# A floor under the issue time of token loads and packed-weight loads, and unpacking two places later, in a one-core attention and FFN layer

## The chip, the cores and the metric

The kernel runs on one core of a Trainium2 chip. The metric is the device time of one execution in microseconds (us). Three runs of the kernel before gave 826.74 us in the median (825.87 to 827.88). PE is the matrix engine (PEld its weight loads), DVE the vector engine, ACT the scalar engine, POOL the general-purpose engine, and SP the queue from which nearly all DMAs of this kernel are issued, in order.

## The reference

The layer takes tokens `x` of 4 batches x 512 positions x 1024 channels and computes, in fp32:

```
x = x + attention(layernorm(x))          # 32 query heads of 32 channels, one shared key/value head
x = x + layernorm(x) @ W.T + bias        # W is 1024 x 1024, stored packed

attention: q = n @ Wq ; k, v = split(n @ Wkv)
           p = softmax(q k^T / sqrt(32) + slope_h * (pos_k - pos_q), causal)
           out = (p v) @ Wo
W:         qweight is int32 [1024, 768]; each group of 3 words gives 4 codes of 6 bits:
           v0 = w0 & 63, v1 = (w0 >> 6) & 63, v2 = w1 & 63, v3 = w2 & 63
           W = (code - zero_point[row]) * scale[row]
```

The packed weights do not depend on the tokens. They are unpacked, turned and written back to device memory (`wf_d`) at any time before the FFN reads them.

## The kernel before

**Stages.** The attention is cut into 32 steps: 4 batches x 8 groups of 4 heads. A step `i` is `queries(at, i)` (24 products `pq`, L682, which use the two-part split of weights and tokens for accuracy), a round trip of the queries through device memory (`q_d`) into a tile `qs` (L697 to L714, all recorded at the helper line L420), `maxima(at, i)` (products `s`, L738, whose row maxima DVE takes at L751 into `mx`), a transpose of the maxima `trm` (L767), two small DMAs of them into `qs` (`qs<-mt`), and `attention(at, i)` (products `st` L819, exponentials on ACT L829, causal masking L838 and sums L860 on POOL, products `pav` L848 and `den` L877). After the steps come 16 token tiles with the output projection (`po` L1047) and the FFN (`pf` L1167).

**Tokens of a batch.** `load_x` brings four tiles of 128 tokens (512 KB each, L554) into the pool `x`, which has 4 buffers. `layernorm` takes their statistics on DVE (L527), the reciprocal root on POOL, and normalizes on ACT (L585, later batches). `chunk` transposes them on PE (L598) and splits them into eight tiles `xc_b_c`, which `keys_values` and all eight `queries` of the batch read. `load_x` of batches 1 to 3 has a nominal place of `T - 45 + 3 t` us, where `T = 16 + 120 b` is that of the batch's first step.

**Unpacking.** `unpack(at, c)` handles 128 rows of the packed weights: a load `qw` (384 KB, L908), three shift/mask operations on DVE (`v`, L912, L919, L926), a conversion on ACT (`code`, L934), a transposing DMA (`across`, L942), another conversion on ACT (`codes`, L945), and a write to `wf_d` (512 KB, L948, recorded at L420). `qw`, `v` and `codes` take buffers of the pool `xc`. That pool has 10 buffers, 8 of which hold the tokens of the current batch, so two are to spare.

**What sets the order.** No order is written out by hand. Every operation is entered with an engine, a modelled cost and a nominal place `at`; `Work.order` then runs a list scheduler over it. A forward pass puts on each engine the ready operation that is wanted first; a DMA is held back until `o.hold`, and from the second pass on also until 12 us (`EARLY`) before the latest time that a backward pass gave it. The backward pass knows nothing of holds, and both passes charge DMAs to a modelled rate. Of 4 rounds of up to 7 forward passes the one with the earliest modelled end wins, and that order is issued on every engine. `o.hold` is 0 except for DMAs issued from POOL, which are held to their `at`. Nominal places, holds and the planned start times are on the planner's clock, which is near the trace's but not the same: the keys and values of batch 1 have the nominal place 135 us and run at 145 us in the trace.

Which buffer a tile takes is decided by `slots`, from the nominal places in the first round and from the planned starts in later rounds. Each engine executes its own list strictly in the planned order, so one late operation holds back all behind it on its engine, SP's DMA issues included.

Of the kernel before, what the change touches and what calls it, by code (L numbers as in the profile page):

```python
# [336 lines left out]
STEP = 15.0  # L337
# [4 lines left out]
def layer_kernel(  # L342
# [14 lines left out]
    nc = tc.nc  # L357
# [3 lines left out]
    NG = NH // GH  # L361
# [4 lines left out]
    work = Work()  # L366
# [14 lines left out]
    def new(pool_name, tag, shape, dt, name):  # L381

        p, bufs = pools[pool_name]
        return work.item(lambda: p.tile(shape, dt, tag=tag, name=name), (pool_name + tag, bufs))
# [13 lines left out]
    def act(at, n, fn, out, ins, sbuf=False):  # L398
        work.op("ACT", at, n / 1.2 + (90.0 if sbuf else 70.0), fn, out, ins)

    def dve(at, n, fn, out, ins, port=False, more=0.0):
        work.op("DVE", at, n / 0.96 + 75.0 + more, fn, out, ins, port=port)
# [1 line left out]
    def pool_op(at, cost, fn, out, ins):  # L404
        work.op("POOL", at, cost, fn, out, ins, port=True)

    def dma(at, size, fn, out, ins, eng="SP"):
        work.op(eng, at, 0.0, fn, out, ins, size=size)

    def split(at, n, hi, lo, src, hi_it, lo_it, src_it, port=False):  # L410

# [7 lines left out]
    def move(dst, src):  # L419
        return nc.sync.dma_start(out=dst.bitcast(F32), in_=src.bitcast(F32))  # L420
# [22 lines left out]
        out=mask(),  # L443
        in_=mask(),
# [14 lines left out]
    def prep_keys(at, i):  # L459
        dma(  # L460
            at, 61e3, lambda: nc.gpsimd.dma_start(out=kst[i]()[R_BIAS:R_ALL, :], in_=k_rows),
            [(kst[i], "b")], [], eng="POOL",
        )

    def prep_rows(at, g):
        dma(
            at, 229e3, lambda: nc.gpsimd.dma_start(out=qr_d[g], in_=q_rows[g]), [qr_i[g]], [],
            eng="POOL",
        )
# [4 lines left out]
    def prep_wkv(at):  # L474
        st = new("stg", "stg", [P, KC, 2 * HD], F32, "wkv_st")
        src = w_kv.rearrange("(c p) d -> p c d", p=P)
        dma(at, 262e3, lambda: nc.sync.dma_start(out=st(), in_=src), [st], [])
        split(
            at + 18.0, HALF, lambda: wkv()[:, :, 0 : 2 * HD], lambda: wkv()[:, :, 2 * HD :], st,
            (wkv, 0), (wkv, 1), st, port=True,  # L480
        )
# [68 lines left out]
    def load_x(at, b, t):  # L550
        xt = xh[b, t] = new("x", "x", [P, H], F32, f"x_{b}_{t}")
        src = x[b, ts(t, P), :]
        if b or t < NT - 1:
            dma(at, 524e3, lambda: nc.sync.dma_start(out=xt(), in_=src), [xt], [])  # L554
            return
        for i in range(2):
            dma(
                at + 0.001 * i, 262e3,
                lambda i=i: nc.sync.dma_start(out=xt()[:, ts(i, HALF)], in_=src[:, ts(i, HALF)]),
                [(xt, i)], [],  # L560
            )
# [342 lines left out]
    def unpack(at, c):  # L904

        qw = new("xc", "xc", [P, H // 4, 3], I32, f"qw_{c}")
        src = qweight[ts(c, P), :].rearrange("p (g w) -> p g w", w=3)
        dma(at, 393e3, lambda: nc.sync.dma_start(out=qw(), in_=src), [qw], [])  # L908
        v = new("xc", "xc", [P, H // 4, 4], I32, f"v_{c}")
        dve(  # L910
            at + 4.0, 256,
            lambda: nc.vector.tensor_scalar(  # L912
                v()[:, :, 0:1], qw()[:, :, 0:1], 63, None, ALU.bitwise_and
            ),
            [(v, 0)], [qw], port=True,
        )
        dve(
            at + 4.0, 256,
            lambda: nc.vector.tensor_scalar(  # L919
                v()[:, :, 1:2], qw()[:, :, 0:1], 6, 63, ALU.logical_shift_right, ALU.bitwise_and  # L920
            ),
            [(v, 1)], [qw], port=True,
        )
        dve(
            at + 4.0, 256,
            lambda: nc.vector.tensor_scalar(  # L926
                v()[:, :, 2:4], qw()[:, :, 1:3], 63, None, ALU.bitwise_and
            ),
            [(v, 2)], [qw], port=True,
        )  # L930
        code = new("stg", "stg", [P, H], BF16, f"code_{c}")
        act(
            at + 5.0, H,
            lambda: nc.scalar.activation(  # L934
                code(), v().rearrange("p g j -> p (g j)"), AF.Copy, bias=-CODE_MID
            ),
            [code], [v], sbuf=True,
        )
        across = new("stg", "stg", [P, KC, P], BF16, f"across_{c}")
        dma(  # L940
            at + 6.0, 700e3,
            lambda: nc.sync.dma_start_transpose(out=across(), in_=code()), [across], [code],  # L942
        )
        turned = new("xc", "xc", [P, KC, P], F32R, f"codes_{c}")
        act(at + 12.0, H, lambda: nc.scalar.copy(turned(), across()), [turned], [across], sbuf=True)  # L945
        dma(
            at + 14.0, 600e3,
            lambda: move(wf_d.rearrange("k p n -> p k n")[:, :, ts(c, P)], turned()),  # L948
            [(wf_i, c)], [turned],
        )  # L950
# [266 lines left out]
    T0 = 16.0  # L1217
    for t in range(NT):
        load_x(0.01 * t, 0, t)
        layernorm(1.0 + t, 0, t)  # L1220
# [4 lines left out]
        prep_wq(2.0 if g == 0 else T0 + (g - 0.9) * STEP, g)  # L1225
        prep_rows(T0 + g * STEP + (2.0 if g == 0 else -6.0), g)
    for c in range(KC):
        unpack(T0 + (1.6 + 2.0 * (c % 3) + NG * (c // 3)) * STEP, c)
    for b in range(B):
        T = T0 + b * NG * STEP  # L1230
        if b:
            for t in range(NT):
                load_x(T - 3.0 * STEP + 3.0 * t, b, t)
            for t in range(NT):
                layernorm(T - 2.0 * STEP + 3.0 * t, b, t)
        for c in range(KC):
            chunk(
                T - 4.0 + 0.5 * c if b == 0 else T - 0.9 * STEP + 1.3 * c - 2.6, b, c
            )
        keys_values(T + 6.0 if b == 0 else T - 1.0, b)  # L1240
        for g in range(NG):
            i = b * NG + g
            at = T0 + i * STEP
            queries(at, i)
            maxima(at + 17.0, i)
            attention(at + 34.0, i)
        invert(T + NG * STEP + 48.0, b)
# [52 lines left out]
```

## Time and profile before

| | |
|---|---|
| median of 3 runs | 826.74 us |
| the profiled execution | 825.42 us |
| its span, first to last instruction | 823.5 us |
| PE busy | 795.9 us (97%) |
| DVE, ACT, POOL busy | 565.5, 372.3, 514.1 us |
| moved by DMA | 133.39 MB, 162 GB/s over the span |
| granted TensorE clock, mean | 0.994 |

The span is the profiled execution from its first to its last instruction; its own time is 1.92 us longer. The chain of waits that ended last goes through PE for 89% of the span. Idle time of PE is therefore what there is to read: 27.6 us in all, and its place in the span tells what would have to arrive earlier. Where two engines, or an engine and the DMAs, run side by side, only the one that PE waits for counts. A granted clock below 1.00 makes PE's products longer without any idle time.

### The profile page before, as it was taken

What the parts mean: (1) busy time and instruction counts of PE and PEld (TensorE: products, weight loads), DVE (VectorE), ACT (ScalarE), POOL (GpSimd) and SP (SyncE); (2) the same over time, 40 slices, a digit from 0 to 9 for tenths busy, and PEclk for the clock granted to TensorE, in tenths of its full rate; (3) what the DMA queues carried; (4) which work ended last, traced back from release to release, by engine and by line L of the source; (5) the groups of instructions that cost most, each with busy time, mean ns of one, the idle gap of its engine ahead of it and who ended that gap; (6) DMA issues with size and microseconds to landing.
All of it is one profiled execution on the core that took longest, in us unless ns stands there. A gap on an engine that the chain in (4) does not pass through costs nothing.

```text
span 823.5 us, 13425 instructions
## 1 busy us (share of the span) xinstructions
PE 795.9 (97%) x4480; PEld 594.7 (72%) x4480; DVE 565.5 (69%) x1491; ACT 372.3 (45%) x659; POOL 514.1 (62%) x442
## 2 busy tenths in 40 slices
PE   5979999999999999999999999999999999999997
PEld 4756676777676767676775767667888888888885
DVE  7476777388786388777367675644998666666865
ACT  4336575464775445675556564330233323332320
POOL 4337977276787375877489896879465445554333
PEclk9989999999999999999999999999999999999999
DMA  7885853395553387543567966526875755665321
GB/s 223 245 252 154 232 164 91 111 266 188 155 145 100 106 262 211 148 120 111 174 174 194 235 189 208 170 58 171 214 178 158 173 131 129 152 151 137 97 52 51
DMA packets 131796, 133.39 MB, mean 162 GB/s; under 512 B 42964, under 2 KB 93140, under 8 KB 130704
## 3 DMA queue, kind: packets, MB, share of 16 engines
q1 hardware_dynamic: 130912, 129.01, 57.0%
q0 software_dynamic: 816, 3.53, 1.7%
q8 instruction: 35, 0.57, 0.3%
q14 instruction: 33, 0.27, 0.1%
HBM read 85.58 MB, written 39.85 MB: 152 GB/s over the span
## 4 chain that ended last, share of the span: by engine, by line
PE 89%; DVE 4%; DMA 2%; ACT 2%; issue 1%; POOL 1%; SPq 1%; DVEq 0%; ACTq 0%; POOLq 0%
PE po L1047 21%; PE pq L682 21%; PE pf L1167 13%; PE st L819 9%; PE s L738 9%; PE pav L848 8%; PE den L877 4%; PE pkv L616 2%; PE tr L598 2%; DVE junk L751 2%; ACT p L829 1%; POOL p L860 1%; DMA wo_st<-in_L_attn_Wo_dram 1%; DMA qs<-mt 1%; SPq L420 1%
## 5 line engine op out<-in xcount | busy, mean ns | idle before, releaser
L751 DVE CUSTOM_DVE_ANT_0 junk<-s,mask 128x384 f32<-128x384 f32 (+3 forms) x512 | 250.6, 490 | 119.6 <-PE s L738 88.8
L860 POOL TENSOR_TENSOR p<-p,p 128x1536 f32<-128x1536 f32 (+2 forms) x96 | 232.4, 2421 | 16.7 <-PE pav L848 15.0
L829 ACT ACTIVATE p<-st 128x512 f32<-128x512 f32 (+1 forms) x352 | 183.9, 559 | 115.8 <-PE st L819 110.7
L682 PE MATMUL pq<-xc,wqh 128*128 128x512 f32 x512 | 198.5, 405 | 2.3 <-DVE ql L415 1.4
L1047 PE MATMUL po<-woh,aT 128*128 128x512 f32 x512 | 164.8, 391 | 0.0
L838 POOL TENSOR_SCALAR_AFFINE_SELECT p<-p 128x512 f32<-128x512 f32 x128 | 82.2, 647 | 105.1 <-ACT p L829 104.3
L738 PE MATMUL s<-kst,qs 124*128 124x384 f32 (+3 forms) x512 | 127.5, 324 | 3.9 <-DVE mx L751 3.6
L819 PE MATMUL st<-qs,kst 126*128 126x512 f32 (+1 forms) x352 | 127.1, 399 | 3.9 <-ACT p L829 2.9
L1167 PE MATMUL pf<-wf,xT 128*128 128x512 f32 x512 | 121.1, 390 | 0.7 <-DVE xT L415 0.7
L738 PEld LDWEIGHTS s<-kst,qs 124*128 124x128 f32 x512 | 91.5, 189 | 34.2 <-DVE mx L751 8.9
L682 PEld LDWEIGHTS pq<-xc,wqh 128*128 128x128 f32 x512 | 97.7, 191 | 23.8 <-issue 2.7
L1047 PEld LDWEIGHTS po<-woh,aT 128*128 128x128 f32 x512 | 96.1, 188 | 21.7 <-DVE mx L751 0.8
L1167 PEld LDWEIGHTS pf<-wf,xT 128*128 128x128 f32 x512 | 95.8, 188 | 20.9 <-DVE xT L415 1.1
L682 PE MATMUL pq<-xc,wql 128*128 128x512 f32 x256 | 101.8, 398 | 0.1
L1047 PE MATMUL po<-wol,aT 128*128 128x512 f32 x256 | 99.7, 389 | 0.0
L819 PEld LDWEIGHTS st<-qs,kst 126*128 126x128 f32 x352 | 63.5, 190 | 25.7 <-ACT p L829 10.8
L848 PE MATMUL pav<-p,kv 128*32 128x512 f32 (+3 forms) x1024 | 79.9, 436 | 0.0
L848 PEld LDWEIGHTS pav<-p,kv 128*32 128x32 f32 x1024 | 29.6, 109 | 48.8 <-issue 37.6
L1187 POOL TENSOR_TENSOR x<-x,y 128x512 f32<-128x512 f32 x30 | 42.7, 1425 | 27.4 <-DVE y L1178 27.4
L1047 PEld LDWEIGHTS po<-wol,aT 128*128 128x128 f32 x256 | 48.1, 188 | 9.6
L538 POOL TENSOR_SCALAR rstd_f<-mv_f 128x1 f32<-128x1 f32 x16 | 3.9, 244 | 81.7 <-DVE mv_f L533 72.7
L682 PEld LDWEIGHTS pq<-xc,wql 128*128 128x128 f32 x256 | 49.2, 192 | 7.2 <-POOL wql L489 0.6
(92 smaller groups left out, 878.6 us busy)
## 6 DMA issues: line engine op xcount, KB each, us to landing
qs<-q_d SPq DMA_DIRECT2D x96, 256.0 KB
x<-_attn_hidden_states_dram SPq DMA_DIRECT2D x31, 512.0 KB
q_d<-qh SPq DMA_DIRECT2D x32, 256.0 KB
q_d<-ql SPq DMA_DIRECT2D x32, 256.0 KB
at_d<-a SPq DMA_DIRECT2D x32, 256.0 KB
raw<-at_d SPq DMA_DIRECT2D x16, 512.0 KB
raw<-rden_d SPq DMA_DIRECT2D x64, 128.0 KB
out_dram<-x SPq DMA_DIRECT2D x32, 256.0 KB
```

Of the source, the lines that this page charges most:

```text
L682: nc.tensor.matmul(pq(), w()[:, c, :], xc[b, c]()[:, s, :], start=(c == 0 and n == 0), stop=(c == KC - 1 and n == 2),)
L738: nc.tensor.matmul(ps()[:, o : o + W], q()[0:R_MAX, at, ts(t, P)], k()[0:R_MAX, :W], start=True, stop=True,)
L751: lambda ps=ps, junk=junk, t=t, h=h, W=W, o=o: nc.vector.tensor_tensor_reduce(out=junk()[:, :W], in0=ps()[:, o : o + W], in1=mask()[:, S - ...
L819: nc.tensor.matmul(ps()[:, place, :], k()[0:R_ALL, ts(j, P)], q()[0:R_ALL, mine, j * P :], start=True, stop=True,)
L829: lambda ps=ps, own=own, j=j: nc.scalar.activation(pr[j]()[:, own, :], ps(), AF.Exp),
L838: nc.gpsimd.affine_select(out=d, in_=d, pattern=[[0, GH], [1, P]], compare_op=ALU.is_ge, fill=0.0, base=0, channel_multiplier=-1,)
L848: nc.tensor.matmul(pav()[ts(h, HD), j * P :], kv[b]()[:, j, HD:], pr[j]()[:, h, :], start=(j == 0), stop=(j == NT - 1), tile_position=(0, ...
L860: nc.gpsimd.tensor_tensor(d, d, pr[j](), ALU.add)
L877: nc.tensor.matmul(d()[ts(h, HD), :], onesel()[:, g, :], pr[0]()[:, h, :], start=(g == 0), stop=(g == NG - 1), tile_position=(0, h * HD),)
L1047: nc.tensor.matmul(po(), aT[s][1]()[:, c, :], w()[:, ts(n, HALF)], start=(c == 0 and m == 0), stop=(c == KC - 1 and m == 2),)
L1167: nc.tensor.matmul(pf(), xT()[:, s, c, :], wf[c]()[:, ts(n, HALF)], start=(c == 0 and s == 0), stop=(c == KC - 1 and s == 1),)
L1187: (nc.vector if last else nc.gpsimd).tensor_tensor(d, d, y(), ALU.add)
```

## The change

`dma` takes an optional `hold`, in us on the planner's clock, before which the planner may not issue it. Two kinds of DMA get one:

- the token tiles of batches 1 to 3: `at - 37.5` us, which is 53.5, 56.5, 59.5 and 62.5 us for batch 1, 173.5 to 182.5 for batch 2, 293.5 to 302.5 for batch 3;
- the packed weights `qw`: `at - 3.0` us.

The nominal places of the eight unpackings are counted from `c + 1` instead of `c`. In steps of 15 us after `T0 = 16` they were 1.6, 3.6, 5.6, 9.6, 11.6, 13.6, 17.6 and 19.6; they become 3.6, 5.6, 9.6, 11.6, 13.6, 17.6, 19.6 and 21.6. The floors of the eight `qw` loads are thus 67, 97, 157, 187, 217, 277, 307 and 337 us. Nothing is added to or taken from the work itself: the same instructions and DMAs are issued. The order in which the planner puts them can change anywhere.

```diff
-    def dma(at, size, fn, out, ins, eng="SP"):
-        work.op(eng, at, 0.0, fn, out, ins, size=size)
+    def dma(at, size, fn, out, ins, eng="SP", hold=None):
+
+        o = work.op(eng, at, 0.0, fn, out, ins, size=size)
+        if hold is not None:
+            o.hold = hold * 1e3
...
         if b or t < NT - 1:
-            dma(at, 524e3, lambda: nc.sync.dma_start(out=xt(), in_=src), [xt], [])
+            dma(
+                at, 524e3, lambda: nc.sync.dma_start(out=xt(), in_=src), [xt], [],
+                hold=at - 2.5 * STEP if b else None,
+            )
             return
...
-        dma(at, 393e3, lambda: nc.sync.dma_start(out=qw(), in_=src), [qw], [])
+        dma(at, 393e3, lambda: nc.sync.dma_start(out=qw(), in_=src), [qw], [], hold=at - 3.0)
...
     for c in range(KC):
-        unpack(T0 + (1.6 + 2.0 * (c % 3) + NG * (c // 3)) * STEP, c)
+        unpack(T0 + (1.6 + 2.0 * ((c + 1) % 3) + NG * ((c + 1) // 3)) * STEP, c)
```

## The prediction

> **What bounds the kernel now.** I read the engine shares first, then the busy time by stretches to find where PE is idle or slow, then who PE waited for, and last the SP queue and the DVE in the stretch that stood out.
>
> ```profile
> PE 795.9 (97%) x4480; PEld 594.7 (72%) x4480; DVE 565.5 (69%) x1491; ACT 372.3 (45%) x659; POOL 514.1 (62%) x442
> ```
>
> PE has 823.5 - 795.9 = 27.6 us without work. In stretches of 6 us the start of the kernel looks like this (each engine's busy time, then the granted PE clock, the DMA share, GB/s):
>
> ```profile
> 28.00:34.00 6.00, 4.55 (x23) 3.43 (x22) 1.07 (x3) 3.24 (x6) 0.48 (x1) 1.00 0.98 237
> 34.00:40.00 6.00, 5.86 (x27) 4.47 (x26) 4.01 (x13) 1.24 (x2) 3.83 (x4) 1.00 1.04 350
> 40.00:46.00 6.00, 2.88 (x14) 1.94 (x14) 5.40 (x23) 1.36 (x3) 1.27 (x1) 0.99 1.08 294
> 46.00:52.00 6.00, 6.00 (x20) 4.87 (x21) 3.16 (x9) 1.77 (x2) 3.80 (x8) 0.73 1.04 332
> 52.00:58.00 6.00, 4.04 (x18) 2.64 (x18) 4.85 (x17) 3.36 (x4) 2.35 (x4) 1.00 0.58 148
> 58.00:64.00 6.00, 5.43 (x20) 4.09 (x19) 4.49 (x20) 2.66 (x5) 0.64 (x1) 0.72 0.58 169
> ```
>
> PE is idle for 1.45 + 0.14 + 3.12 + 1.96 + 0.57 = 7.24 us between 28 and 64 us, and two stretches run at a clock of 0.73 and 0.72, which lengthens their products by (0.27 + 0.28) x 6 = 3.30 us. Together 10.54 us. From 28 to 52 us the DMA engines are full. Of the rest of the idle time some 8 us lie before the first product, 5.5 us after 800 us (neither is touched), and about 5 us are spread over 64 to 580 us in waits of at most 0.8 us.
>
> ```profile
> PE st L819 <- ACT p L829: 2.6, 7, 0.5
> PE trm L767 <- DVE xc L415: 0.8, 2, 0.5
> PE st L819 <- DMA qs<-mt: 0.8, 1, 0.8
> ```
>
> So a moved DMA can win only in the first 64 us, and can lose anywhere later. This is SP's list in the full stretch (start, duration of the issue):
>
> ```profile
> 33.86 0.43 SPq L554 DMA_DIRECT2D x<-_attn_hidden_states_dram  x1
> ...
> 35.25 0.98 SPq L554 DMA_DIRECT2D x<-_attn_hidden_states_dram  x2
> ...
> 40.50 0.38 SPq L420 DMA_DIRECT2D wf_d<-codes  x1
> 41.36 4.31 SPq L908 DMA_DIRECT2D qw<-in_L_ffn_qweight_dram  x1
> 45.76 0.54 SPq L507 DMA_DIRECT2D wq_st<-in_L_attn_Wq_dram  x1
> 46.40 1.70 SPq L420 DMA_DIRECT2D q_d<-qh  x1
> 48.19 0.42 SPq L420 DMA_DIRECT2D q_d<-ql  x1
> 48.70 1.25 SPq L420 DMA_DIRECT2D qs<-mt  x2
> ```
>
> The reader should see three token tiles of batch 1 (1.5 MB, not normalized by ACT before 49 us, not transposed before some 110 us), a write of unpacked codes (0.5 MB), and a packed load whose issue blocks SP for 4.31 us. Behind them stand the queries and maxima that PE needs: the maxima were ready on DVE at 46.5 us, were issued at 48.70, and the first `st` product ran at 57.93.
>
> **The change, part by part.** *Which floors bind.* The packed loads are issued at 5.3, 41.4, 83.7, 160.3, 193.9, 216.7, 290.0 and 322.1 us; the floors are 67, 97, 157, 187, 217, 277, 307 and 337. The first two move by 62 and 56 us, the third by 73, the rest by 15 to 60. Token tiles of batch 1 are issued at 33.9, 35.3, 35.7 and 71.2 against floors of 53.5 to 62.5, so three move by 20 to 24 us. Batches 2 and 3 (issued 167 to 197 and 291 to 310) have floors at most 7 us later than that: no effect worth a number.
>
> *What leaves the first 64 us.* Unpacking 0 takes with it the SP issues of 3.29, 1.73 (transposing DMA at 24.79) and 0.38 us, three DVE operations (20.11 to 23.58), and 2.1 us of ACT; unpacking 1 its issue of 4.31 us and 1.2 us of DVE at 62; the three token tiles 1.4 us of SP issue, about 4 us of statistics on DVE between 41.5 and 49, 3 us on POOL, and 3.6 us of ACT. In bytes: 0.77 MB packed, 0.25 MB transposed, 0.5 MB of codes, 1.5 MB of tokens, some 3 of the 14.4 MB that move before 60 us.
>
> *What then comes sooner.* The low part of the first queries (`ql`) waits behind the DVE unpacking: its ACT half is done at 22.42, it starts at 23.50. That is 1.1 us. Its path to `qs` is behind the 1.73 us transposing issue and in a stretch with a DMA share of 0.98. The first `s` product ran at 34.62. It cannot run before the keys are copied, at 30.17 (ACT, 29.58 + 0.58), so the gain there is at most 34.62 - 30.2 = 4.4 us; I take most of it. The PE wait at 31.7 (1.45 us) then has `s` products to fill it. DVE needs 9.9 us for sixteen maxima (35.06 to 45.0), so these end near 41 instead of 45. The small DMAs of the maxima took 4.8 us on the chain of waits in a later stretch (318.44, 4.82); from an issue at 42 that makes the first `st` at about 47, not 57.9. Until then PE has the products of queries 2 and 3 (5.5 us each) and of two sets of maxima.
>
> *What stays.* While no `st` is there, PE runs at DVE's pace: five waits on the maxima between 53 and 60 us (0.53, 0.34, 0.55, 0.54, 0.54) sum to 2.50 us. I keep 2.50 as idle, and one of the two slow-clock stretches (1.65). Gain at the start: 10.54 - 2.50 - 1.65 = 6.4 us; its ends are 0 (DVE bounds the fill as now, below) and 10.54.
>
> *What it costs later.* The same work now lies beside full PE work. One unpacking is 2.3 us of SP issue (0.64 + 1.28 + 0.40), 2.2 us of DVE in the median (single operations up to 3.70 us at 165 us, beside POOL), and 2.1 us of ACT; DVE is 69% and ACT 45% busy, so this is hidden as long as no maxima or queries queue right behind it. Rows for it exist: 300 to 340 us holds a packed load, three token tiles and a transposing DMA, and PE loses 1.46 us there, against 0.0 to 0.5 in its neighbours. Bounds: nothing, or less than nothing since three unpackings leave places where a `st` waits now, to eight times the 0.81 us wait for the maxima's DMA at 323 = 6.5 us. I take 1.0, since the stretches from 140 to 260 us, which hold three unpackings, lose 0.48 + 0.04 + 0.41 = 0.93 in all. If the cover goes (a maxima operation behind a 3.7 us DVE operation), one such event costs up to 3 us.
>
> *Sum.* 6.4 - 1.0 = 5.4 us. The profiled execution of 825.42 us (span 823.5 + 1.92) would become 820.0; it stands 1.32 below the median of the runs, so the forecast is 826.74 - 5.4 = **821.3 us**.
>
> *Two rules against the rows.* The Trainium skill, "DMA: Bandwidth & Descriptors", section "Rules for kernel authors", advises to issue a DMA early and wait late so that its cost overlaps; by it the early loads are free, the gain is nothing, and only the cost of 1.0 us is left: 827.7. The 4.31 us issue and the share of 1.04 to 1.08 speak against it here. "TensorE: Matmul & The Clock Gate", Part 1, has the clock halve after an idle window of about 3.4 us; the waits of 40 to 46 us are 1.68 us at the longest, and the clock still fell to 0.73. By the rule no clock loss could be won back and the forecast would be 1.65 us higher, 823.0.
>
> **The rivals.** *DVE bounds the fill.* For: in the 40 to 46 stretch DVE is 5.40 of 6 us busy and every PE wait there names the maxima. Against: DVE is idle for 5 of 6 us from 28 to 34, so a start 4 us sooner costs it nothing. Then only the 1.45 us wait goes, 1.0 is paid later: 826.3.
>
> *The last unpacking meets the batch switch (slower).* Unpacking 7 takes 35.7 us from load to write now (322.05 to 357.78). From its floor of 337 it ends at 373 or later, holding one or two of the ten `xc` buffers, while the tokens of batch 3 are turned into theirs from 356 and 369.6 to 389. If a `chunk` copy waits for that write, the queries of step 24 wait behind it on PE, which has at most a step's rest to do. The same can befall unpacking 4 at the switch near 255. Price: 8 us (8 of the 16 us of overlap); 826.74 - 5.4 + 8 = 829.3. It decides for slower from a wait of 7.1 us on. Against: the places of 5.6 and 13.6 steps already hold unpackings before two switches, with no wait on PE above 0.4 us at either.
>
> *The floors do nothing.* Excluded: eleven of the twenty floors lie 15 us or more beyond the present issues.
>
> *A new order with more small waits.* The planner re-sorts everything. Its present order loses 5 us from 64 to 580 us; twice that eats the gain: 826.3, three times it: 831.
>
> **How the numbers follow.** Forecast 60%, DVE-bound fill 14%, batch switch 16%, small waits 10%. Under 0.2% (1.65 us) a measurement of this kernel cannot be told from no change. Of the DVE-bound case a third is a small gain, a half the same; of the small waits a third is the same and the rest slower. Faster 0.66, same 0.11, slower 0.23. The forecast alone spans 816.2 (all of 10.54) to 824.5; for 8 in 10 it reaches from 816 to 830, past the batch switch's 829.3.
>
> **What would show it.** Right: no L554 and no L908 on SP between 6 and 50 us; first `s` near 30 to 31 us, first `st` before 50; PE idle of 28 to 64 us under 4 us; later stretches within 1 us of these. Wrong: the first `st` still after 55 (the fill is not the DMAs'); PE waits of several us on `xc` or `tr` near 256 or 376; new DVE waits of 3 us behind L919 after 64 us.

## The result and the profile after

The changed kernel takes 829.80 us in the median (15 runs) against 827.63 us of the kernel before beside it. The ratio is 1.0039, 95% interval 1.0020 to 1.0058: slower by some 3 us, where 821.3 us was forecast. (The ratio is estimated from all runs; that of the two medians alone is 1.0026.) The profiled execution took 831.88 us (span 829.6). Single executions of one kernel scatter by several us (the kernel before from 824.55 to 830.00), so in what follows the traces give the place of a loss and the intervals its size.

The engine shares of the kernel after:

```profile
PE 801.0 (97%) x4480; PEld 596.9 (72%) x4480; DVE 571.4 (69%) x1491; ACT 368.9 (44%) x659; POOL 517.0 (62%) x442
```

The busy time by stretches of the kernel after (PE, PEld, DVE, ACT and POOL with their counts, then the granted PE clock, the DMA share and GB/s):

```profile
28.00:34.00 6.00, 5.05 (x26) 4.01 (x25) 1.93 (x4) 1.81 (x6) 0.37 (x1) 1.00 1.02 234
34.00:40.00 6.00, 6.00 (x31) 5.10 (x30) 4.70 (x19) 1.02 (x2) 3.04 (x3) 1.00 0.85 241
40.00:46.00 6.00, 4.37 (x15) 2.12 (x13) 4.89 (x21) 1.78 (x4) 1.13 (x1) 0.85 0.57 172
46.00:52.00 6.00, 5.45 (x14) 3.93 (x15) 4.80 (x20) 0.20 (x1) 1.42 (x2) 0.50 0.65 171
52.00:58.00 6.00, 6.00 (x25) 4.79 (x25) 1.73 (x8) 2.76 (x6) 0.40 (x1) 0.80 0.63 175
58.00:64.00 6.00, 6.00 (x37) 3.80 (x36) 4.07 (x10) 4.37 (x10) 3.57 (x6) 1.00 0.42 132
64.00:80.00 16.00, 16.00 (x103) 11.34 (x101) 14.00 (x54) 10.11 (x19) 14.74 (x15) 1.00 0.82 260
80.00:100.00 20.00, 17.93 (x113) 10.74 (x113) 12.07 (x47) 12.58 (x25) 19.78 (x19) 1.00 0.74 191
```

```profile
460.00:500.00 40.00, 37.89 (x233) 25.19 (x235) 26.17 (x86) 21.64 (x42) 35.71 (x26) 0.96 0.85 218
500.00:540.00 40.00, 38.02 (x229) 27.73 (x222) 22.56 (x66) 13.89 (x29) 30.26 (x22) 0.96 0.54 178
540.00:580.00 40.00, 38.33 (x210) 27.83 (x209) 20.88 (x25) 10.49 (x19) 31.75 (x26) 1.00 0.43 115
580.00:640.00 60.00, 58.76 (x263) 48.18 (x263) 49.47 (x61) 17.67 (x22) 31.85 (x25) 1.00 0.75 189
```

A stretch's loss is what PE lacks of its length, plus its length times what the clock lacks of 1. From these rows and the same rows of before:

| stretch, us | before: idle + slow clock | after | difference |
|---|---|---|---|
| 0 to 28 | 9.15 | 8.80 | -0.35 |
| 28 to 64 | 7.24 + 3.30 | 3.13 + 5.10 | -2.31 |
| 64 to 100 | 0.49 | 2.07 | +1.58 |
| 100 to 460 | 3.66 | 2.02 | -1.64 |
| 460 to 640 | 1.07 | 7.00 + 3.20 | +9.13 |

The sum is +6.4 us, and the two spans differ by 6.1. What lies behind 640 us is not in the table: there before loses 5.98 us idle and 1.4 to a clock of 0.94, after 5.53 and 0.3, so the whole account comes to some 4.9 us and leaves 1.2 open. (The execution of after that was profiled lies 2.1 us above its median and that of before 2.2 below its own, so the medians' 2.2 us is less than the traces show.) The DMA share in the first 60 us fell as foreseen. The idle time there fell by 4.1 us, but the slow clock gave 1.8 us back, and from 460 to 640 us, where attention hands over to the output projection and the FFN, a new loss stands that nothing in the change aims at. That place is called the handover below. The two longest waits of PE in the kernel after from 64 to 100 us, and then the three longest from 460 to 640 us (us in total, times, longest):

```profile
PE den L883 <- POOL p L866: 1.0, 1, 1.0
PE s L744 <- DVE mx L757: 0.9, 3, 0.3
```

```profile
PE po L1053 <- DVE x L1063: 2.4, 2, 1.2
PE s L744 <- DMA qs<-q_d: 2.1, 1, 2.1
PE s L744 <- DMA qs<-qr_d: 2.0, 1, 2.0
```

Before had three waits of 1.0 us together in the last stretch. From 80 to 100 us POOL is busy for 19.78 of 20 us (before: 18.57), and one of its sums (L866) comes 1.0 us late for PE.

SP's list of the kernel after shows that the early loads did leave; these are the first token tiles of batch 1 and the first packed load (start, duration of the issue):

```profile
52.29 0.50 SPq L558 DMA_DIRECT2D x<-_attn_hidden_states_dram  x1
65.65 0.90 SPq L558 DMA_DIRECT2D x<-_attn_hidden_states_dram  x2
66.59 0.43 SPq L914 DMA_DIRECT2D qw<-in_L_ffn_qweight_dram  x1
```

Now two views of the kernel *before* that the prediction did not put beside its DMA rows. The waits of PE from 28 to 64 us:

```profile
PE s L738 <- DVE mx L751: 3.6, 7, 0.9
PE trm L767 <- DVE mx L751: 1.7, 1, 1.7
PE pq L682 <- DVE ql L415: 1.4, 1, 1.4
PE pq L682 <- ACT mt L773: 0.3, 1, 0.3
```

None of them names a DMA. And the timelines of PE, where the second set of `s` begins, of DVE there, and of PE around its first `st` (start, duration, idle time before it and what ended it):

```profile
51.60 0.63 PE L738 MATMUL s<-kst,qs 124*128 124x512 f32 x2
```

```profile
52.04 0.69 DVE L751 CUSTOM_DVE_ANT_0 junk<-s,mask 128x512 f32<-128x512 f32 x1 [2.87 <-PE s L738]
```

```profile
57.59 0.50 PE L738 MATMUL s<-kst,qs 124*128 124x384 f32 x2 [0.54 <-DVE mx L751]
57.93 0.68 PE L819 MATMUL st<-qs,kst 126*128 126x512 f32 x2
```

The first `st` has no wait of its own. It stands behind the `s` products of the second set in PE's order, and those wait for DVE. DVE had finished the first sixteen maxima at 45.1 us and took none until 52.04, because PE's order put the next `s` at 51.60, with no wait before it. In the kernel after the second set follows much sooner, and DVE goes on with its maxima at 43.46 without a gap:

```profile
42.32 0.50 PE L744 MATMUL s<-kst,qs 124*128 124x512 f32 x1 [0.54 <-DVE mx L757]
```

So the idle time at the start was won through PE's order. The order did it only where the packed loads had left too, as the experiments below show.

### The profile page after: what moved, and what is told of

Its sections match the earlier page's. It is cut to its first block, busy times and chain, and to the rows that moved or that the text cites. A ratio compares the mean times of both kernels' runs of the same rounds, so it can differ in the third digit from the quotient of the medians.

```text
span 829.6 us, 13411 instructions
## 1 busy us (share of the span) xinstructions
PE 801.0 (97%) x4480; PEld 596.9 (72%) x4480; DVE 571.4 (69%) x1491; ACT 368.9 (44%) x659; POOL 517.0 (62%) x442
## 4 chain that ended last, share of the span: by engine, by line
PE 81%; DVE 7%; DMA 5%; POOL 3%; issue 2%; ACT 1%; SPq 1%; DVEq 0%; POOLq 0%; ACTq 0%
PE pq L688 20%; PE po L1053 18%; PE pf L1173 11%; PE st L825 9%; PE s L744 8%; PE pav L854 8%; PE den L883 3%; DVE junk L757 3%; PE tr L604 2%; PE pkv L622 2%; DMA raw<-rden_d 1%; DVE x L1155 1%; DMA qs<-q_d 1%; DMA qs<-qr_d 1%; DMA x<-_attn_hidden_states_dram 1%
## 5 line engine op out<-in xcount | busy, mean ns | idle before, releaser
L866 POOL TENSOR_TENSOR p<-p,p 128x1536 f32<-128x1536 f32 (+2 forms) x96 | 231.4, 2410 | 15.3 <-PE pav L854 13.8
L688 PE MATMUL pq<-xc,wqh 128*128 128x512 f32 x512 | 200.7, 407 | 0.0
L844 POOL TENSOR_SCALAR_AFFINE_SELECT p<-p 128x512 f32<-128x512 f32 x128 | 84.6, 666 | 112.5 <-ACT p L835 108.5
L744 PE MATMUL s<-kst,qs 124*128 124x384 f32 (+3 forms) x512 | 129.6, 329 | 8.8 <-DVE mx L757 3.4
L825 PE MATMUL st<-qs,kst 126*128 126x512 f32 (+1 forms) x352 | 125.1, 399 | 0.9 <-ACT p L835 0.6
L744 PEld LDWEIGHTS s<-kst,qs 124*128 124x128 f32 x512 | 93.3, 193 | 41.1 <-issue 11.9
L1155 DVE SCALAR_TENSOR_TENSOR x<-rows,sumx,x 128x512 f32<-128x512 f32 x32 | 53.1, 1686 | 1.8 <-POOL x L1151 0.6
L1151 POOL TENSOR_TENSOR x<-x,rows 128x512 f32<-128x512 f32 x32 | 42.8, 1358 | 17.3 <-DVE x L1074 9.0
```

The lines of the kernel that those rows point to most:

```text
L688: nc.tensor.matmul(pq(), w()[:, c, :], xc[b, c]()[:, s, :], start=(c == 0 and n == 0), stop=(c == KC - 1 and n == 2),)
L744: nc.tensor.matmul(ps()[:, o : o + W], q()[0:R_MAX, at, ts(t, P)], k()[0:R_MAX, :W], start=True, stop=True,)
L825: nc.tensor.matmul(ps()[:, place, :], k()[0:R_ALL, ts(j, P)], q()[0:R_ALL, mine, j * P :], start=True, stop=True,)
L844: nc.gpsimd.affine_select(out=d, in_=d, pattern=[[0, GH], [1, P]], compare_op=ALU.is_ge, fill=0.0, base=0, channel_multiplier=-1,)
L866: nc.gpsimd.tensor_tensor(d, d, pr[j](), ALU.add)
L1151: nc.gpsimd.tensor_tensor(d, d, rows["bias"][n][1](), ALU.add)
```

## The experiments

Two theories were put against each other. Theory R: the loss is in the re-sorted order, in work that no floor touches. Its rival (theory L in the expectations): the moved work itself costs where it now stands. All ratios are to the kernel before, run beside.

| kernel | ratio, 95% interval |
|---|---|
| changed order to 420 us, then before's | 1.0010 (0.9997 to 1.0023) |
| before's order to 420 us, then the changed | 1.0062 (1.0048 to 1.0075) |
| the same joins at 250 us | 1.0085 (1.0064 to 1.0106) and 1.0029 (1.0014 to 1.0043) |
| before's order, moved work alone | 1.0043 (1.0029 to 1.0056) |
| token tiles alone | 1.0044 (1.0029 to 1.0058) |
| token tiles alone, normalized still later | 1.0029 (1.0016 to 1.0043) |
| unpackings alone | 0.9990 (0.9977 to 1.0003) |
| second bank for a query product | 0.9995 (0.9977 to 1.0012) |
| unpackings alone and second bank | 0.9982 (0.9967 to 0.9996) |
| another order of the kernel before | 1.0084 (1.0064 to 1.0104) |
| the change with 24 planner rounds | 1.0052 (1.0033 to 1.0072) |
| floor on tokens only, planned | 1.0035 (1.0018 to 1.0051) |
| floor on weights only, planned | 1.0130 (1.0113 to 1.0147) |

### Joined orders: which part of the span loses

Both plans are made in one kernel, and the instructions of one up to a cut are joined to the rest of the other. Every engine runs the joined list. The place of the cut is called the seam.

```diff
-    ordered = work.order()
+    work.order()
+    late = [o.start for o in work.ops]     # with the floors and later places
...
+    work.order()
+    soon = [o.start for o in work.ops]     # without them
+    CUT = 420e3
+    ordered = sorted(
+        work.ops,
+        key=lambda o: (soon[o.n] > CUT, (soon if soon[o.n] > CUT else late)[o.n], o.n),
+    )
```

That is the changed order first. For the converse `soon` and `late` change places in the key.

> The changed kernel's order for every operation that the planner of before starts by 420 us on its clock (all loads under a floor and seven of eight unpackings and more lie there), the order of before for everything later. Theory R (the re-sorted handover): the moved work costs little where it now lies, and the loss is in the order around 460 to 640 us; so the 9 us lost there go and the start's gain stays: 825.0 us (822 to 827.5), and no idle of PE above 0.6 us between 460 and 640 us. Theory L (the late loads cost): the moved work is still late, so 829 to 831 us.

Measured: 827.84 against 827.39 us, between what the two theories expected. The start is that of the changed kernel, 3.22 us idle and 5.04 us of slow clock from 28 to 64 us, and 2.13 us are lost from 64 to 100 us. The trace also shows 5.0 us idle from 420 to 500 us, right behind the seam. The gain of the start does not reach the end, and whether the seam took it this run alone does not show.

> The reverse: the order of before up to 420 us on the planner's clock, that of the changed kernel later. No load is held back and no unpacking is later (only the last write of codes stays early). Theory R: the handover of the changed kernel is lost on top of the slow start: 834 to 837 us, with waits of about 2 us on the query DMAs near 477 and 508 us. Theory L: nothing is late, so the time of before, 827.6 us.

Measured: 833.37 us, +0.62%. Up to 420 us this kernel runs before's order. The waits of PE from 460 to 640 us:

```profile
PE s L745 <- DMA wo_st<-in_L_attn_Wo_dram: 2.8, 1, 2.8
PE po L1054 <- DVE x L1064: 2.4, 2, 1.4
PE st L826 <- ACT p L836: 1.9, 3, 1.2
```

The changed order costs 5 us here with every load before 420 us at its old place. The 2.4 us on `po` are as in the changed kernel. The wait for `wo_st` is in neither parent, so a part of the 5 us could be the seam's. That was tried last, with the seam at 250 us:

```diff
-    CUT = 420e3
+    CUT = 250e3
```

> The order of before up to 250 us as planned, the changed order from there on; the same join as h2_before_then_changed (833.4, +6.0 us), but with its seam at 250 instead of 420 us. If the loss belongs to the changed order of the stretch after 420 us, it stays: 831.5 to 834.5, with PE idle of some 6 to 9 us between 460 and 640 us, and little in 240 to 280. If it belonged to the seam, it moves there or goes: PE idle of 3 us or more between 240 and 280 us, under 3 us between 460 and 640, and a time that is set by how this seam falls, 826 to 830.

Measured: 828.18 us, +0.29%, less than expected if the loss were all the order's. The idle time from 460 to 640 us is 5.40 us (0.58, 1.73, 1.69 and 1.40 in the four stretches shown above), against 1.07 in before, with 2.7 us in waits for `DVE x L1064` and no wait for `wo_st`. So a loss at the handover comes with the changed order from 250 us on, the last unpackings at their later places included. The whole kernel lost 2.4 us (1.2 to 3.6) by the interval, and the other 2.7 us or so of the first join would be its seam's.

> The changed order up to 250 us as planned, the order of before from there on; the same join as h1_changed_then_before (827.8, +0.4 us), whose trace showed 2.55 us idle at 420 to 460 and 2.48 at 460 to 500 us. If those 5 us were the seam's, they go, and the rest is the start's gain (4 us idle won in 28 to 64 less 1.6 to 2 lost in 64 to 100): 824.5 to 826.5. If they came with work that stands later because the start was changed, they stay: 827 to 829.

Measured: 832.39 us, +0.85%, against both theories. This seam brought a loss of its own, much like the rival of the prediction in which an unpacking meets a batch switch. The timelines of ACT and of PE:

```profile
260.81 1.06 ACT L941 ACTIVATE code<-v 128x1024 bf16<-128x1024 int32 x1 [1.55 <-DVE v L933]
265.00 1.04 ACT L952 CAST codes<-across 128x1024 fp32r<-128x1024 bf16 x1 [3.13 <-DMA across<-code]
265.95 0.59 ACT L836 ACTIVATE p<-st 128x512 f32<-128x512 f32 x1
266.44 0.58 ACT L416 CAST xc<-tr 128x512 fp32r<-128x512 f32 x1
```

```profile
267.80 0.95 PE L605 MATMUL tr<-ident,x 128*128 128x128 f32 x4 [4.73 <-DVE xc L419]
```

In this order the second conversion of an unpacking stands on ACT right behind the first. ACT waits 3.13 us for the transposing DMA between them, and the copy `xc<-tr` of the next batch's tokens stands behind it. PE lost 4.73 us, and a granted clock of 0.96 over the 40 us took 1.6 more. The prediction looked for this through the buffers of `xc`; it came through ACT's queue (the last copy into `xc`, on DVE at 267.05, had to wait for that one).

### The moved work alone, in the order of before

Here the planner's order of before is kept, and only the moved operations get other places in it. The three token tiles of batch 1 with their statistics and normalization go 20 us later. Each unpacking takes the places of the next one, the last goes to 380 to 405 us, and the first packed load to 52 us.

```diff
+    place = {o.n: o.start for o in work.ops}
+    moved = dict(place)
+    for c in range(KC - 1):
+        for o, p in zip(marks["u", c], marks["u", c + 1]):
+            moved[o.n] = place[p.n]
+    moved[marks["u", 0][0].n] = 52e3
+    for o, t in zip(marks["u", KC - 1], (380, 389, 389.4, 390, 391.5, 393, 399, 405)):
+        moved[o.n] = t * 1e3
+    for t in range(3):
+        for o in marks["x", 1, t]:
+            moved[o.n] = place[o.n] + 20e3
+    ordered = sorted(work.ops, key=lambda o: (moved[o.n], o.n))
```

> The order of before on every engine, with only these operations taken out and put in later: three token tiles of batch 1 with their statistics and normalization 20 us later; the first packed load at 52 us; unpackings 0 to 6 in the places of 1 to 7; unpacking 7 at 380 to 405 us. Nothing else is re-sorted. The prediction's step (the full DMA engines hold up the first queries): first s product at 30 to 31 us, first st product before 50 us, 820 to 823 us. Rival (DVE bounds the fill): 825.5 to 827. Theory L: 829 or more.

Measured: 830.74 us, +0.43%. This speaks against R as the whole cause: the moved work does cost in an order that was not re-sorted. The start won nothing. The first `s` ran at 34.72 (before: 34.62), the first `st` at 57.49, and idle and slow clock from 28 to 64 us were 7.04 + 3.24, with no packed or token load issued between 6 and 47 us. From 64 to 100 us PE sat idle for 3.11 us instead of 0.49. The two halves of the edit were then tried one by one.

> The order of before, with only the unpackings moved (0 to 6 in the places of 1 to 7, 7 at 380 to 405 us, first packed load at 52 us). If the unpacking is what costs: 829 to 831 us. If the tokens are: 827 to 828 us. In both cases the start up to 64 us stays as before, with the first s product within 0.3 us of 34.6.

Measured: 825.68 against 826.46 us, no difference that can be told from zero. The first `s` ran at 33.97, a little sooner than expected. At these places later unpackings cost nothing and win nothing that the runs can tell.

> The order of before, with only the three token tiles of batch 1 and their statistics and normalization put in 20 us later. The move of all the work together cost 3.4 us (0.43%), most of it between 64 and 100 us, where PE lost 3.1 us instead of 0.5. If the tokens' ACT and DVE work among the first exponentials is the cause: 829 to 830.5 us, with waits of PE on the exponentials near 70 to 82 us. If it is the unpacking: 827 to 828 us.

Measured: 830.34 us, +0.44%: all of the loss of the two together is the tokens'. The timelines of POOL, ACT and PE in this kernel:

```profile
70.29 3.51 POOL L866 TENSOR_TENSOR p<-p,p 128x1536 f32<-128x1536 f32 x1
73.77 0.23 POOL L541 TENSOR_SCALAR rstd_a<-mv_a 128x1 f32<-128x1 f32 x1
74.08 0.57 POOL L546 TENSOR_TENSOR rstd_a<-rstd_a,neg_half 128x1 f32<-128x1 f32 x1
74.76 0.27 POOL L584 TENSOR_SCALAR nmr<-mv_a,rstd_a 128x1 f32<-128x1 f32 x1
```

```profile
75.06 1.24 ACT L591 ACTIVATE x<-x,nmr,rstd_a 128x1024 f32<-128x1024 f32 x1 [2.81 <-POOL nmr L584]
76.21 0.56 ACT L415 CAST qh<-pq 128x512 fp32r<-128x512 f32 x1
76.68 1.09 ACT L835 ACTIVATE p<-st 128x512 f32<-128x512 f32 x2
```

```profile
77.33 1.18 PE L825 MATMUL st<-qs,kst 126*128 126x512 f32 x2 [1.63 <-ACT p L835]
```

The small operations of a normalization (0.23, 0.57 and 0.27 us) stand on POOL behind a sum of 3.51 us. ACT, in its order, waits 2.81 us for their result, and the exponentials that PE needs stand behind ACT's normalization. In before POOL was done with these tiles at 52.6 us, and its first sum came at 70.39. The loss from 64 to 100 us is 2.72 us idle plus 1.80 us of slow clock.

If ACT's wait were all of it, normalizing later still, when POOL's result is long there, would win it back:

```diff
     for t in range(3):
         for o in marks["x", 1, t]:
-            moved[o.n] = place[o.n] + 20e3
+            moved[o.n] = place[o.n] + (36e3 if o.eng == "ACT" else 20e3)
```

> As the tokens alone (20 us later), with the normalizations on ACT 36 us later than before in place of 20. In the run of the tokens alone ACT stood 2.81 us at 72 to 75 us for a small POOL operation that is queued behind a POOL sum of 3.5 us, and the exponentials behind it on ACT made PE wait 1.63 us. If that in-order wait is the cost: the PE wait near 77 us goes, PE idle of 64 to 100 us falls from 2.7 to under 1.2 us, and the time is 826.5 to 828.5 us. If the tokens' work on POOL and DVE is the cost wherever ACT stands: 829.5 to 831 us as with the tokens alone.

Measured: 828.82 us, +0.29%, between the two expected ranges. The wait of 1.63 us went, but `den` waited 0.9 us for POOL's sums, `st` 1.1 us for ACT and `s` 0.5 for DVE, and the idle time from 64 to 100 us stayed at 2.60 us. The intervals of this kernel and of the last overlap. So ACT's wait was one form of the loss and not all of it. What stays is that the tokens' work on POOL, ACT and DVE costs at both places tried; which of the three engines sets the price was not shown.

### What sets the start

The 1.4 us wait for `ql` is a product `pq` waiting until DVE has emptied the one bank in which PE adds up the queries. The third set of queries (step 2) was given a bank of the scores instead:

```diff
+        if i == 2:
+            pq.make = lambda: pools["ps_st"][0].tile([P, S], F32, tag="st", name="pq_2")
```

> The order and all loads of before; only the third set of query products goes to one of the two st banks, which nothing uses before the first st, in place of the one query bank. Theory O (the order on PE and the one query bank set the start, not the DMAs): the wait of 1.45 us at 31.7 us is gone, the first s product runs at 33.2 to 33.4 us though all early loads are still in front, and the time is 825 to 827.4 us. Theory D (the full DMA engines hold up the first queries): the first s product stays at 34.6 us or names a DMA as what it waited for, and the time is that of before.

Measured: 825.68 against 826.46 us, the same. The waits of PE from 28 to 64 us:

```profile
PE s L740 <- DVE mx L753: 3.4, 6, 0.9
PE s L740 <- DMA qs<-q_d: 2.2, 1, 2.2
PE trm L769 <- DVE mx L753: 1.7, 1, 1.7
```

The wait for the bank is gone, and a wait for the queries' DMA of 2.2 us has come right behind it; the first `s` ran at 35.00. So there seem to be two gates in series: the bank, and the DMAs that the prediction had blamed. Then both were opened, the bank as here and the unpackings moved as above (tokens at their old places):

> The order of before with the unpackings moved as before (tokens left early), and the third set of query products in an st bank. With the bank alone PE met a second gate at once: the first s product waited 2.21 us for the queries' DMA and ran at 35.0 us. Theory of two gates in series (order and bank, then the early DMAs): with both taken away the first s product runs at 32.5 to 33.5 us and idle of 28 to 64 us falls by 1 to 3 us; 823.5 to 825.5 us. Theory DVE (the maxima on DVE set the pace whatever comes sooner): s is sooner, but the idle of 28 to 64 us stays within 1 us of 7.2, and the time is that of before.

Measured: 824.40 against 826.58 us, ratio 0.9982 (0.9967 to 0.9996), the one version whose interval lies below 1. (It overlaps with those of the two halves, 0.9990 and 0.9995, so the gain of both over one alone is not shown by the times.) The first `s` ran at 32.58 and the first `st` at 55.25, and the maxima were issued 4.6 us sooner (44.11 against 48.70). The waits of PE from 28 to 64 us:

```profile
PE s L746 <- DVE mx L759: 3.8, 7, 0.9
PE trm L775 <- DVE mx L759: 1.7, 1, 1.7
```

Of four waits the two on DVE's maxima are left, at 5.5 us. In before's order no version lost them: they are 4.2 to 5.5 us in the traces of all of these.

The idle time of PE from 28 to 64 us sorts the versions, each by one trace. With before's order of the start it is 6.4 to 8.6 us, whether loads were moved or not, and 5.53 with bank and unpackings. New orders with the packed loads still early have 6.52 (floor on tokens only, where one wait for `qs<-q_d` is 3.1 us) and 6.91 (another order of before). New orders with the packed loads late have 3.13, 3.22 and 4.43 (the changed order, alone and joined), 3.73 (floor on weights only) and 4.24 (24 rounds). So in these traces neither the later packed loads nor a new order won the start alone; the two together did.

### What a re-sorted order is worth

The planner keeps the best of 28 passes by its own model. Here the kernel before takes the last pass instead; no place and no floor is changed.

```diff
+            last = (end, start)
...
-        self.end, start = best
+        self.end, start = last
```

> The kernel before with no floor and no place changed; only the order that the last of the planner's 28 forward passes gave is issued in place of the best one (its modelled end is 808.1 us against 805.9; the changed kernel's best is 808.3). If the search's luck is worth as much as the change: 828.5 to 832 us, a difference of 0.2 to 0.5% with not one load moved by a floor. If orders near the best are worth the same: 827 to 828 us.

Measured: 834.26 us, +0.84%. The waits of PE from 64 to 600 us:

```profile
PE s L739 <- DVE mx L752: 3.0, 1, 3.0
PE po L1048 <- DVE x L1058: 2.7, 1, 2.7
```

The `po` wait of the handover is there with no load moved. In this one order a re-sorting alone cost twice the whole effect of the change. The converse, letting the planner search longer on the changed kernel (`work.order(rounds=24)`):

> The changed kernel with a longer search: 24 rounds of the planner in place of 4, whose best modelled end is 805.9 us as for the kernel before (808.3 with 4 rounds). Floors and places are those of the change. Theory R (the loss is in which order the search happened on): 825 to 828 us. Theory L: 829 to 831 us, as the floors are unchanged.

Measured: 831.27 us, +0.52%, with 3.42 us idle and 3.24 us of slow clock from 64 to 100 us. An order that the planner's model prefers to that of the changed kernel (by the expectation, 805.9 us against 808.3) was no faster. Two more, each with one half of the change, planned anew:

```diff
# the first: floors on the token tiles only
+                hold=at - 2.5 * STEP if b else None,
# the second: floors and later places of the packed weights only
+        dma(at, 393e3, lambda: nc.sync.dma_start(out=qw(), in_=src), [qw], [], hold=at - 3.0)
...
+        unpack(T0 + (1.6 + 2.0 * ((c + 1) % 3) + NG * ((c + 1) // 3)) * STEP, c)
```

> Of the change only the floor on the token tiles; the planner orders anew. It models an end of 804.9 us, the best of all versions (before 805.9, changed 808.3). If the planner's end tells orders apart by 2 us: 825 to 827 us. If the tokens cost where they are put, as in the run of the tokens alone: 829 to 831 us, with PE idle of 64 to 100 us above 2 us.

Measured: 828.93 us, +0.35%, with 1.64 us idle from 64 to 100 us and a wait of 3.8 us for `po` at the handover.

> Of the change only the floor on the packed weights and their later places; the tokens may be loaded as early as before; the planner orders anew and models an end of 810.4 us, the worst of all versions. If the planner's end tells orders apart: 831 to 834 us. If the moved unpacking is free, as in the run of the unpacking alone, and orders differ by chance only: anywhere from 826 to 832 us.

Measured: 836.77 us, +1.30%, the slowest of all, although its start is good (first `s` at 32.29, first `st` at 53.56, 3.73 us idle from 28 to 64). From 340 to 380 us it loses 4.83 us idle and 3.6 us to a clock of 0.91. The timelines of POOL, DVE and ACT, and the wait of PE there:

```profile
364.84 5.90 POOL L866 TENSOR_TENSOR p<-p,p 128x1536 f32<-128x1536 f32 x2 [0.26 <-PE pav L854]
```

```profile
365.11 3.46 DVE L925 TENSOR_SCALAR v<-qw 128x256 int32<-128x256 int32 x1
368.42 2.60 DVE L932 TENSOR_SCALAR v<-qw 128x512 int32<-128x512 int32 x1
```

```profile
371.05 1.06 ACT L940 ACTIVATE code<-v 128x1024 bf16<-128x1024 int32 x1 [6.69 <-DVE v L932]
372.01 0.24 ACT L779 CAST mt<-trm 16x128 fp32r<-16x128 f32 x1
```

```profile
PE tr L604 <- DVE mt L784: 4.8, 1, 4.8
```

Two operations of an unpacking ran on DVE beside two sums of POOL and took 3.46 and 2.60 us. In the kernel joined at 250 us the same two took 0.43 us each (at 260.09 and 260.35), while POOL was idle. ACT, in its order, stood 6.69 us for them with the unpacking's conversion; behind that conversion stood the small copy `mt`, whose second part DVE made at 372.28, and behind that PE. This is the event that the prediction priced at up to 3 us if the cover of an unpacking goes. So unpackings cost nothing that the runs can tell at the places tried by hand, and cost PE 4.8 us where one falls beside POOL's sums with a small operation behind it.

All five newly planned orders, the changed kernel's included, are slower than before's, by 0.35 to 1.30%. By the modelled ends that the expectations give, the one that the model likes least (810.4 us) is the slowest, but one with the same end as before (805.9) lost 0.52%: orders that the model holds equal lie 4 us apart.

## Why the prediction was wrong

**The early loads hold up the first queries: wrong as put.** This is the step that failed: the gain of 6.4 us at the start was put on the DMAs alone. The prediction followed the full DMA engines and SP's 4.31 us issue, and left the waits of the stretch, which name DVE and ACT alone, to a rival. The unpackings moved alone gave 0.9990 with the first `s` at 33.97; tokens and unpackings together gave it at 34.72, no sooner than before, with 7.04 us idle at the start instead of 7.24. The DMAs are a second gate, seen at 35.00 once the bank is free. With bank and unpackings both moved the first `s` is 2 us sooner and the kernel 0.18% faster.

**The low part of the first queries waits behind DVE's unpacking, 1.1 us: read rightly, but it was not what held `s` up.** With the work moved in before's order that `ql` started at 22.55 instead of 23.50, right behind its ACT half, and the first `s` still ran at 34.72. In PE's order it stands behind products of the third set of queries, and those wait 1.4 us for the `ql` of the second set (DVE, 32.39 in before). That wait stayed with the unpacking gone and went with a second bank.

**First `s` at 30 to 31, first `st` before 50: missed.** They came at 32.94 and 53.93. The first bound (the copy of the keys to `kst`) was named rightly but came later itself, since the new order put it at 32.31 instead of 29.58: `s` at 32.94 waits 0.95 us for it. The `st` step failed in its reading: the interval from the maxima's issue (48.70) to `st` (57.93) was taken as a DMA's delay, but `st` stood behind second-set `s` products that wait for DVE. Hence the maxima issued 4.6 us sooner with bank and unpackings moved `st` by 2.7 only, and with the unpackings alone, issued 3.2 us sooner, not at all (58.66).

**What stays at the start, 2.50 idle and 1.65 slow clock: the idle time near by chance, the clock wrong.** 3.13 and 5.10 us were measured, so the start won 2.3 us and not 6.4. The 2.50 were waits on maxima with no `st` there; of the 3.13 some 2.0 wait on maxima and 0.95 on the keys. In kernels with before's order of the start the clock took 3.24 us in one trace, 5.04 in the kernel with token tiles alone and 5.76 in the order joined at 250 us; a gain of 1.65 us out of one trace's clock cannot be counted on.

**The cost later, 1.0 us: mis-sized, and for the wrong work.** It was priced for unpackings, which in before's order cost nothing that the runs can tell (0.9990). The three token tiles, whose 4 us on DVE, 3 on POOL and 3.6 on ACT the prediction listed only as leaving the start, cost 0.44%, 3.6 us (2.4 to 4.8), where they arrive in before's order. No row was sought for their new place, where POOL runs 3.5 us sums.

**DVE bounds the fill (a rival at 14%): right for before's order.** There the waits that no version lost are those on DVE's maxima. What that rival missed is that a re-sorted order, with the packed loads gone, could fill DVE's gap of 45 to 52 us, which gave the 4.1 us of idle time.

**A new order with more small waits (a rival at 10%): this came, and was held too unlikely.** The rival's two ends were 826.3 and 831 us, and 829.8 was measured. From 64 to 580 us PE was indeed idle for 9.9 us instead of 5.2, but this gathers at the handover, it is less than before from 100 to 460 us, and the clock falls with it. Since nothing in the profile of before prices a new order, and another order of the same work differed by 0.84%, a change whose floors make the planner sort 4,480 PE instructions anew should have carried this as its main case.

**The unpacking meets the batch switch (16%): not in the changed kernel.** No wait of several us on `xc` or `tr` appeared. In the order joined at 250 us a like event cost PE 4.7 us and 1.6 of slow clock, less than the 8 us priced.

A ledger in the sizes of the runs: 2.4 us for the order after 250 us and 3.6 us for the tokens, less 2.3 us of the start, makes 3.7 us, against 3.2 us by the measured ratio. This is an estimate, and the agreement may be chance: the three do not come from one kernel, and the 2.3 us come from single traces. In the changed kernel's own traces the difference is +1.6 us from 64 to 100 us and +9.1 at the handover.

**The two rules.** The advice of the Trainium skill to issue a DMA early and wait late ("DMA: Bandwidth & Descriptors", "Rules for kernel authors") was set aside for the full queue. It speaks of the fixed setup cost of a DMA, and the runs decide only in part: in before's order the early packed loads cost nothing that the times tell (0.9990 with them moved), but with the bank free they are a gate of 2.2 us. The 0.44% of the token tiles does not bear on it, since their statistics and normalization moved along. The rule on the clock ("TensorE: Matmul & The Clock Gate", Part 1, an idle window of about 3.4 us) does not by itself account for what the rows show: in the kernel after the clock was 0.50 from 46 to 52 us, and no single wait in the 18 us before the end of that stretch was over 0.54 us.

**What stays open.** Which instruction of the changed order makes the handover worse was not found. Three of the four joins show a loss of their own at or behind the seam, so the split between the order and the moved work rests on the tokens alone and on before's order joined to the changed one at 250 us; both intervals are 2.4 us wide.

## What to carry to other kernels

Read who PE waits for in the very stretch before blaming a full DMA engine; a wait that names another engine can stay when the DMA goes, and an instruction that is late without a wait of its own stands behind others in its engine's order. When work is moved out of a bad place, price it at its new place on every engine that it touches, the small operations on a busy in-order engine above all. Where a change makes a planner sort everything anew, first measure what another order of the same work costs, and if the gain sought is smaller than that, move the work by hand in the old order.

## What the runs showed of the hardware

The clock fell to 0.50 in a stretch with 0.55 us idle, after one with 1.63 us idle in pieces of at most 0.54 us; no long wait stood before it. A shift and mask of 128x256 integers took 0.43 us on DVE with POOL idle, and 3.46 us beside POOL's sums of 128x1536. SP's issue of the 384 KB packed load took 4.31 us at a DMA share of 1.08 (40 to 46 us) and 0.43 us at 66.59 in the kernel after, at a share of 0.82. The share does not explain this: with the token tiles alone moved, and so no longer issued ahead of it, the same load was issued in 0.65 us at 38.73, at a share of 1.12 from 38 to 44 us.
